# The first query weights between two blocks of x, and the last heads counted between products: one change to a gated attention kernel

## The chip, the core and the metric

The kernel runs on one core of one Trainium2 chip. The core has five engines with instruction queues of their own: TensorE (PE, with its weight loads as PEld), VectorE (DVE), ScalarE (ACT), GpSimd (POOL) and SyncE (SP, which here does nothing but issue transfers). The metric is the device time of one execution in microseconds (us), median of the runs. A profiled execution has a span, from the first to the last recorded instruction, and a little time around it that belongs to the device time too.

## What is computed

One transformer block over x of 2 x 1024 tokens and 512 features. x is normalized; 32 heads of 16 features attend causally; a base projection with a routed low-rank part (8 experts of rank 16, the best 2 of them) makes a gate; the output is x plus the product of both.

```python
xn = _layernorm(x, axis=-1)
s = _L0_attn_ref(xn, Wq, bq, Wk, bk, Wv, bv, Wo, bo)   # causal softmax attention, 32 heads of 16, then Wo
g = _silu(_L0_ffn_ref(xn, W_base, b_base, W_gate, A, B))  # base + top-2 of 8 rank-16 experts
x = x + s * g
```

## The kernel before

**Two programs in one.** `attn_gated_block` (line 79) runs `direct`, a fast path that is right as long as the softmax sums and their reciprocals stay in range. `direct` counts how many of these checks hold and leaves the count as an integer in `sound`, one number in on-chip memory. Line 93 then loads it into a register of every engine (`values_load`, one TENSOR_LOAD on each of the five queues, each waiting for `sound`), and line 94 compares it and branches: with the full count, as here, all engines jump over `general`, a slower and long program that stands between the branch and the end. The code that follows the jump is that of the end of the kernel (line 2176 in the profile): every engine drains, then they meet.

**Tiling.** Tokens are handled in chunks of C = 512 (two for each of the two sequences), each in four blocks of P = 128 tokens. Weights and heads are handled in four groups of 128 features. A unit is one sequence, one group of eight heads and one chunk of queries: 16 units, each a row of steps of scores (line 1607), exponentials (line 1618), masks on POOL (line 1635) and value products (line 1659). The steps are in `plan`, and the loop from line 1694 writes them out. `fill` puts projection work between them, from a list of tasks with costs and due times. The order on every engine is written out by this program (`manual_schedule`); each engine runs its own list strictly in order. That order is the same before and after the change, apart from what is named below.

**The start.** `x_first` holds the first four blocks of x. Lines 133 and 134 issue their loads on SP, then line 179 calls `load_qk(0)`, which loads the first group of query weights (wq) and of key weights (wk), then wv, bv and the second group follow. `first_task` (line 354) handles the four blocks: `statistics` (bn_stats, bn_aggr and a sum on DVE, a power on POOL), `normalize` on DVE, `turn` (four transposes on PE into one PSUM tile, one copy of 128 x 512 by ACT, lines 364 to 373), `project_first` (line 375, four products with wq or wk for one block). DVE's order is: statistics of blocks 0 and 1, normalize 0, statistics of 2, normalize 1, statistics of 3, normalize 2, normalize 3. PE's is: turn 0, the bias rows, queries of block 0, turn 1, keys of block 0, turn 2, queries of 1, turn 3, queries of 2 and 3, keys of 1, then the first scores. 

**The end.** The last unit ends with the last 128 queries (t = 3). `post_tile` (line 1124) transposes their heads (`pt_o`), divides by the softmax sums (`olast`) and leaves the reciprocals in `rc_last`. `turn_last` (line 1163) transposes the heads back (`pt_y`) and ACT copies them into `oT`. `whole_task` (line 1199) makes the output projection of a block, four groups k of four products with wo; `third`, the last task of this kind, does it for t = 2. `rest_task` (line 1221) does what is left for t = 3: range check into `fine`, the last group of products (line 1227), then the count: a product of `fine` with a column of ones (`pn`, line 1232), a sum and a cast to `sound` on DVE (lines 1235 and 1236). `finish_tile` (line 1192) multiplies with the gate and adds the base, both on DVE, and issues the store on SP. The end is written out in lines 1708 to 1717:

```python
    third.step()
    turn_late()
    rest.step()
    while third in tasks:
        third.step()
    active.clear()
    while late or turns or tasks:
        fill(last + 99)
```

Of the kernel before, what the change touches and what calls it, by code (L numbers as in the profile page):

```python
# [8 lines left out]
F32 = mybir.dt.float32  # L9
# [4 lines left out]
ALU = mybir.AluOpType  # L14
AX = mybir.AxisListType
# [3 lines left out]
P = 128  # L19
# [7 lines left out]
KC = D // P  # L27
# [5 lines left out]
NF = 2 + 4 * 2 * 4  # L33
# [44 lines left out]
@with_exitstack  # L78
def attn_gated_block(ctx: ExitStack, tc: tile.TileContext, *args):

    nc = tc.nc
    flag = ctx.enter_context(tc.tile_pool(name="flag", bufs=1))
    sound = flag.tile([1, 1], I32, name="sound")  # L90
    with ExitStack() as direct_ctx:
        direct(direct_ctx, tc, sound, *args)
    n = nc.values_load(sound[0:1, 0:1])
    with tc.If(n < P * NF, preferred_fallthrough_block=False):
        with ExitStack() as general_ctx:
            general(general_ctx, tc, *args)


def direct(ctx, tc, sound, x, wq, wk, wv, wo, wb, wa, wg, wB, bq, bk, bv, bo, bb, out):
# [9 lines left out]
    nc = tc.nc  # L109
    ve = Metered(nc.vector, 0.19, 966)  # L110
    act = Metered(nc.scalar, 0.22, 1274)
    sp = Queue(nc.sync)
    NB, L, _ = x.shape
    C = 512
    NC = L // C
    TT = C // P

    ctx.enter_context(tc.manual_schedule(engines=ENGINES))
    cst = ctx.enter_context(tc.tile_pool(name="cst", bufs=1))
# [5 lines left out]
    ps_av = ctx.enter_context(tc.tile_pool(name="ps_av", bufs=2, space=PSUM))  # L125
# [4 lines left out]

    x_first = chunk_tile(0, 0)
    first = [x_first[:, t] for t in range(TT)]
    for t in range(TT):
        sp.dma_start(out=first[t], in_=x[0, t * P : (t + 1) * P, :])

    def load_qk(oc):


        t = sb.tile([P, 4 * KC, P], F32, tag="wqk", bufs=2, name=f"wqk{oc}")
        for n, src in enumerate((wq, wk)):  # L140
            sp.dma_start(
                out=t[:, (2 + n) * KC : (3 + n) * KC],
                in_=src.rearrange("(kc p) o -> p kc o", p=P)[:, :, oc * P : oc * P + P],
            )
        return t

    def pair_up(t):
# [28 lines left out]
    b_rows = sb.tile([2 * KC, P], F32, tag="hl", bufs=1, name="b_rows")  # L176
    nc.scalar.dma_start(out=b_rows[0:KC], in_=bq.rearrange("(kc p) -> kc p", p=P))
    nc.scalar.dma_start(out=b_rows[KC : 2 * KC], in_=bk.rearrange("(kc p) -> kc p", p=P))
    wqks = [load_qk(0)]
    wv_sb = load_whole(wv, "wv")  # L180
    bv_sb = load_b(bv, "bv_sb")
    wqks.append(load_qk(1))
# [45 lines left out]
        rev, pattern=[[-1, E]], base=E, channel_multiplier=0,  # L228
        allow_small_or_imprecise_dtypes=True,
    )  # L230
    ones = cst.tile([P, 1], F32, name="ones")
    nc.gpsimd.memset(ones, 1.0)

    W = C // HD
# [3 lines left out]
    MM = 0.853  # L238
# [8 lines left out]
    def mm_tile(name):  # L247
        return ps_mm.tile([P, D], F32, tag="mm", name=name)
# [31 lines left out]
    def normalize(xs, mv, rstd):  # L280
        for t, xt in enumerate(xs):
            ve.tensor_scalar(
                xt, xt, mv[:, t, 0:1], rstd[:, t : t + 1], ALU.subtract, ALU.mult
            )
# [69 lines left out]
    def first_task():  # L354

        xnT = sb.tile([P, KC, C], F32, tag="xnT", bufs=3, name="xnT_0_0")
        qT = sb.tile([P, 2, C], F32, tag="qT", bufs=2, name="qT_0_0_0")
        kT = sb.tile([P, C], F32, tag="kf", bufs=2, name="kf_0_0_0")
        xnTs[0, 0], qTs[0, 0, 0] = xnT, qT
        kfs.append(kT)  # L360
        pq = ps_av.tile([P, C], F32, tag="av", name="pq_first")
        pk = ps_av.tile([P, C], F32, tag="av", name="pk_first")

        def turn(t):
            pt = mm_tile("pt_x")
            for k in range(KC):
                nc.tensor.transpose(
                    pt[:, k * P : (k + 1) * P], first[t][:, k * P : (k + 1) * P], ident
                )
            act.copy(  # L370
                xnT[:, :, t * P : (t + 1) * P], pt.rearrange("p (k t) -> p k t", k=KC)
            )
            turned_at[0, 0] = now[0] - 5

        def project_first(ps, w, t):
            cols = slice(t * P, (t + 1) * P)
            for k in range(KC):
                nc.tensor.matmul(  # L378
                    ps[:, cols], lhsT=w[:, k, :], rhs=xnT[:, k, cols], start=k == 0, stop=k == KC - 1
                )  # L380

        def queries(par):
            ve.tensor_scalar(
                qT[:, par], pq, bq_sb[:, 0:1], half[:, par : par + 1], ALU.add, ALU.mult
            )

        def keys(t0, t1):
            cols = slice(t0 * P, t1 * P)
            act.activation(kT[:, cols], pk[:, cols], AF.Identity, bias=bk_sb[:, 0:1])

        def transform(t, s):
            normalize(first[t : t + 1], *s)
            turn(t)

        s0 = yield from statistics(first[0 : 1])
        s1 = yield from statistics(first[1 : 2])
        transform(0, s0)
        b_ps = mm_tile("b_ps")[:, 0 : 2 * KC]
        nc.tensor.transpose(b_ps, b_rows, ident[0 : 2 * KC, 0 : 2 * KC])
        act.copy(b_sb, b_ps)  # L400
        s2 = yield from statistics(first[2 : 3])
        project_first(pq, wqks[0][:, 2 * KC : 3 * KC], 0)
        transform(1, s1)
        s3 = yield from statistics(first[3 : 4])
        project_first(pk, wqks[0][:, 3 * KC :], 0)
        transform(2, s2)
        project_first(pq, wqks[0][:, 2 * KC : 3 * KC], 1)
        transform(3, s3)
        room["x"] += 1
        keys(0, 1)  # L410
        project_first(pq, wqks[0][:, 2 * KC : 3 * KC], 2)
        project_first(pq, wqks[0][:, 2 * KC : 3 * KC], TT - 1)
        queries(0)
        queries(1)
        ve.stream_shuffle(b_pair, b_sb, PAIRED)
        ve.tensor_tensor(b_less, b_pair[:, 0:KC], b_pair[:, KC:], ALU.subtract)
        project_first(pk, wqks[0][:, 3 * KC :], 1)
        yield 6 * MM
        project_first(pk, wqks[0][:, 3 * KC :], 2)
        project_first(pk, wqks[0][:, 3 * KC :], 3)  # L420
        keys(1, TT)
        kTs[0, 0, 0] = sb.tile([P, 2, C], F32R, tag="kT", bufs=4, name="kT_0_0_0")
        low = sb.tile([P, C], F32, tag="rb", bufs=1, name="low_0_0_0")

        def apart():
            ve.stream_shuffle(low, kT, PAIRED)
            split_keys(kTs[0, 0, 0], low, low)
            later.append((now[0] + 1, lambda: place_keys(kTs[0, 0, 0], low)))

        later.append((0, lambda: pair_up(wqks[1])))  # L430
        paired = lambda: pair_up(wqks[0])
        costs[paired], costs[apart] = (1.1, 5), (1.1, 6)
        later.append((3, paired))
        later.append((4, apart))
        yield 2 * MM
# [49 lines left out]
    def split_keys(kT, kf, low):  # L485

        act.activation(kT, kf.unsqueeze(1).to_broadcast([P, 2, C]), AF.Copy)
        ve.tensor_tensor(low, kf, kT[:, 0].bitcast(F32), ALU.subtract)
# [663 lines left out]
    turns, turned, posts, posted, later, patient, last_out = [], [], {}, [], [], [], []  # L1152
# [16 lines left out]
    bases, whole_wo, splits, costs, urgent = {}, [], [], {}, []  # L1169
# [19 lines left out]
            ve.scalar_tensor_tensor(y, bo_sb[:, 0:BK], 0.5, g[:, BK:D], ALU.mult, ALU.mult)  # L1189
            ve.tensor_tensor(right, right, y, ALU.add)  # L1190

    def finish_tile(b, c, t, po):
        i = c * TT + t
        y = gs.pop((b, i))
        ve.scalar_tensor_tensor(y, po, 0.5, y, ALU.mult, ALU.mult)
        ve.tensor_tensor(y, y, bases[t], ALU.add)
        sp.dma_start(out=out[b, i * P : (i + 1) * P, :], in_=y)

    def whole_task(b, c, t, hold=0):

        while t not in turned or normalized(b, c) < KC - 1:
            yield WAIT
        while now[0] < hold:
            yield WAIT
        po = mm_tile("po")
        for _ in project_out(po, b, c, t, 0, KC):
            yield MM
        finish_tile(b, c, t, po)
        yield MM

    def most_task(b, c, t):
# [9 lines left out]
    def rest_task(b, c, t):  # L1221

        list(last_in_range())
        while t not in turned:
            yield WAIT
        po = mm_tile("po")
        matmul(
            po, lhsT=oTs[b, c][:, KC - 1, t * P : t * P + P], rhs=whole_wo[0][:, KC - 1],
            start=True, stop=True,
        )  # L1230
        pn = mm_tile("pn")[0:1, 0:NF]
        nc.tensor.matmul(pn, lhsT=ones, rhs=fine, start=True, stop=True)
        finish_tile(b, c, t, po)
        count = small.tile([1, 1], F32, tag="count", bufs=1, name="count")
        ve.tensor_reduce(count, pn, AX.X, ALU.add)
        ve.tensor_copy(sound, count)
        yield MM


    def in_range(ok, flat, low, high):  # L1240
# [5 lines left out]
    fine = small.tile([P, NF], F32, tag="fine", bufs=1, name="fine")  # L1246
# [123 lines left out]
    for b in range(NB):  # L1370
        for c in range(NC):
# [70 lines left out]
            else:  # L1442
                before = starts[b, KC - 1, c] + 2
                Task(len(plan) - 7, bases_task(b, c), 0.0, after=before - 12, takes={"xnT": 2})
                n = len(units) - 3
# [262 lines left out]
    third = next(x for x in tasks if x.begun)  # L1708
    rest = next(x for x in tasks if x is not third)
    third.step()  # L1710
    turn_late()
    rest.step()
    while third in tasks:
        third.step()
    active.clear()
    while late or turns or tasks:
        fill(last + 99)


def general(  # L1720
# [459 lines left out]
```

## Time and profile before

| | us |
|---|---|
| median of 3 runs | 550.99 |
| lowest, highest | 550.79, 551.87 |
| the profiled execution, device time | 551.06 |
| its span | 549.3 |
| PE, ACT, DVE, POOL busy in the span | 536.8, 351.5, 333.3, 116.6 |
| PE busy from 0 to 12 us | 9.40 |
| PE busy from 536 to 543 us | 4.83 |
| PE busy from 543 us to the end (549.3) | 0 |

The rows by stretch show where PE isn't busy: in the first 12 us it is idle for 2.6 us, in the last 13.3 us for 8.5 us, and in the 524 us between it is idle for some 1.4 us. The granted TensorE clock is 1.00 in every stretch up to 543 us. A row of the timeline gives the start (us from the span's start), the duration, engine, source line, operation and tiles; in brackets stands the idle time before it and what ended it. DVE, ACT and most POOL work shows line 56, since a helper records it; it is told apart by its tiles. The profile has 98% of the span as PE busy, where the ends of products are modelled.

### The profile page before, as it was taken

What the parts mean: (1) busy time and instruction counts of PE and PEld (TensorE: products, weight loads), DVE (VectorE), ACT (ScalarE), POOL (GpSimd) and SP (SyncE); (2) the same over time, 40 slices, a digit from 0 to 9 for tenths busy, and PEclk for the clock granted to TensorE, in tenths of its full rate; (3) what the DMA queues carried; (4) which work ended last, traced back from release to release, by engine and by line L of the source; (5) the groups of instructions that cost most, each with busy time, mean ns of one, the idle gap of its engine ahead of it and who ended that gap; (6) DMA issues with size and microseconds to landing.
All of it is one profiled execution on the core that took longest, in us unless ns stands there. A gap on an engine that the chain in (4) does not pass through costs nothing.

```text
span 549.3 us, 19455 instructions
## 1 busy us (share of the span) xinstructions
PE 536.8 (98%) x8411; PEld 278.4 (51%) x8411; DVE 333.3 (61%) x693; ACT 351.5 (64%) x389; POOL 116.6 (21%) x248
## 2 busy tenths in 40 slices
PE   8999999999999999999999999999999999999993
PEld 7435444554455544454555554454545554456651
DVE  4435586665575975566378766675086544649833
ACT  2437754776776867657666756657668776876640
POOL 2213401020134411030124321030123332020500
PEclk9999999999999999999999999999999999999998
DMA  8724357356527376713646635641133212642211
GB/s 255 187 91 158 143 161 233 98 176 196 174 98 230 126 232 217 214 42 104 210 137 195 207 111 185 186 137 45 47 111 119 82 65 54 240 157 82 97 41 47
DMA packets 66798, 78.11 MB, mean 142 GB/s; under 512 B 9880, under 2 KB 51872, under 8 KB 66064
## 3 DMA queue, kind: packets, MB, share of 16 engines
q1 hardware_dynamic: 66688, 76.78, 43.7%
q8 instruction: 68, 1.11, 0.9%
q14 instruction: 26, 0.21, 0.2%
q10 hardware_dynamic: 16, 0.00, 0.0%
HBM read 45.34 MB, written 19.37 MB: 118 GB/s over the span
## 4 chain that ended last, share of the span: by engine, by line
PE 94%; DVE 2%; ACT 1%; DMA 1%; issue 0%; SPq 0%; ACTq 0%; DVEq 0%
PE av L1659 26%; PE p L253 23%; PE s L1607 18%; PE q L253 14%; PE ph L253 3%; PE pv L253 3%; PE po L253 3%; PE pk L253 1%; PE pq L253 1%; ACT pt L56 1%; DMA wqk<-in_wq_dram 1%; PE pq_first L378 1%; PE h L253 1%; DVE g L56 1%; PE pk_first L378 1%
## 5 line engine op out<-in xcount | busy, mean ns | idle before, releaser
L56 ACT ACTIVATE pt<-s 128x1024 f32<-128x1024 f32 x288 | 290.3, 1025 | 152.0 <-PE s L1607 144.4
L1635 POOL TENSOR_SCALAR_AFFINE_SELECT pt<-pt 128x256 f32<-128x256 f32 (+1 forms) x224 | 108.6, 501 | 406.5 <-ACT pt L56 405.8
L1659 PE MATMUL av<-pt,v 128*32 128x512 f32 (+3 forms) x1680 | 155.8, 467 | 0.4 <-DVE v L56 0.2
L1607 PE MATMUL s<-qT,kT 32*128 32x512 f32 (+3 forms) x1616 | 108.3, 363 | 0.7 <-ACT pt L56 0.5
L1607 PEld LDWEIGHTS s<-qT,kT 32*128 32x128 f32 x1616 | 62.1, 183 | 59.4 <-issue 34.0
L1659 PEld LDWEIGHTS av<-pt,v 128*32 128x32 f32 x1680 | 41.1, 108 | 54.6 <-issue 38.4
L253 PE MATMUL p<-wt,asum 128*32 128x256 f32 x864 | 52.6, 379 | 0.0
L253 PE MATMUL q<-asum,wqk 128*32 128x256 f32 x832 | 51.1, 379 | 0.0
L253 PEld LDWEIGHTS p<-wt,asum 128*32 128x32 f32 x864 | 28.5, 110 | 26.4 <-issue 11.2
L253 PE MATMUL q<-xnT,wqk 128*32 128x256 f32 x624 | 39.5, 379 | 0.0
L253 PEld LDWEIGHTS q<-asum,wqk 128*32 128x32 f32 x832 | 26.8, 110 | 23.7 <-issue 7.2
L56 DVE TENSOR_TENSOR g<-p,g 128x512 f32<-128x512 f32 x20 | 13.8, 690 | 26.6 <-PE p L253 26.5
L253 PEld LDWEIGHTS q<-xnT,wqk 128*32 128x32 f32 x624 | 20.2, 110 | 18.5 <-issue 6.6
L56 DVE SCALAR_TENSOR_TENSOR kf<-q,kf 128x256 f32<-128x256 f32 x39 | 16.5, 424 | 21.3 <-PE q L253 20.6
L253 PE MATMUL p<-w,xnT 128*32 128x256 f32 x448 | 27.4, 379 | 0.0
L253 PE MATMUL p<-w,asum 128*32 128x256 f32 x320 | 20.8, 379 | 0.0
L253 PEld LDWEIGHTS p<-w,xnT 128*32 128x32 f32 x448 | 14.9, 110 | 10.6 <-issue 3.3
L253 PEld LDWEIGHTS ph<-wag_sb,xnT 128*32 128x32 f32 x512 | 15.3, 110 | 3.9 <-issue 3.0
L253 PE MATMUL po<-wo,oT 128*32 128x512 f32 x128 | 16.5, 593 | 0.4 <-ACT oT L56 0.4
L253 PE MATMUL ph<-wag_sb,xnT 128*32 128x136 f32 x512 | 16.7, 279 | 0.0
L56 DVE TENSOR_TENSOR x<-p,x 128x512 f32<-128x512 f32 x15 | 10.3, 687 | 10.3 <-PE p L253 10.2
L56 DVE TENSOR_TENSOR qT<-qf,qT 128x512 fp32r<-128x512 f32 x15 | 10.4, 697 | 9.4 <-ACT qT L56 9.4
(149 smaller groups left out, 564.8 us busy)
## 6 DMA issues: line engine op xcount, KB each, us to landing
wt<-kept SPq DMA_DIRECT2D x36, 256.0 KB
qT<-qT SPq DMA_DIRECT2D x30, 256.0 KB
x<-in_x_dram SPq DMA_DIRECT2D x16, 256.0 KB
kept<-wqk SPq DMA_DIRECT2D x16, 256.0 KB
wqk<-kept SPq DMA_DIRECT2D x4, 1024.0 KB
kT<-kf SPq DMA_DIRECT2D x30, 128.0 KB
scr<-sq SPq DMA_DIRECT2D x6, 512.0 KB
xnT<-scr SPq DMA_DIRECT2D x24, 128.0 KB
```

The costliest lines, as they stand in the source:

```text
L56: return getattr(self.engine, name)(*args, **named)
L253: nc.tensor.matmul(o[j : j + 32], lhsT=lhsT[:, j : j + 32] if len(lhsT.shape) == 2 else lhsT[:, j // 32], rhs=rhs, start=start, stop=stop,)
L378: nc.tensor.matmul(ps[:, cols], lhsT=w[:, k, :], rhs=xnT[:, k, cols], start=k == 0, stop=k == KC - 1)
L1607: nc.tensor.matmul(ss[s // 2][:, s % 2, col : col + w], lhsT=keys[rows, kt % TT * P : kt % TT * P + P], rhs=q[rows, halves * par + half_, ...
L1635: nc.gpsimd.affine_select(out=d, in_=d, compare_op=ALU.is_ge, fill=0.0, base=0, pattern=[[0, d.shape[1]], [1, P]], channel_multiplier=-1,)
L1659: nc.tensor.matmul(avs_now[par][32 * s : 32 * s + 32, q0 : q0 + w], lhsT=vs[b, kt][:, h * VS - HD * par : h * VS - HD * par + HP], rhs=pt[ ...
```

## The change

It has five edits, all in `direct` and its caller.

1. **Start, loads.** The loads of x are issued as blocks 0 and 1, then wq, then blocks 2 and 3, then wk. The rest of SP's list is as it was.
2. **Start, first turn.** For block 0 the copy by ACT is made in two halves of 128 x 256, each issued after two of the four transposes. On PE the third transpose then waits for the first half's copy, as both use one PSUM tile.
3. **End, order on PE.** After the value products, `third` makes its third group of products (k = 2), then the last heads are turned (`pt_y`), then the count is made by the new `count_fine`, then `third` makes its last group (k = 3), then the last group of t = 3. Before it was: k = 2, k = 3, turn, last group of t = 3, count. The product with ones has 32 columns of ones in place of one, and its result stands in a tile of the value products' PSUM pool; sum and cast on DVE come before the two `finish_tile`.
4. **End, loading the count.** `values_load` stands in `rest_task` ahead of its `finish_tile`, no longer behind everything. So each queue has the TENSOR_LOAD earlier: DVE between the multiplications of t = 2 and t = 3, SP between the stores of t = 2 and t = 3, PE behind its last product, ACT behind its last copy, POOL behind the sum of edit 5. The comparison and the branch stay where they were.
5. **End, one sum.** The last addition of t = 2 in `finish_tile` is made by POOL in place of DVE; the store of t = 2 waits for POOL.

```diff
-        direct(direct_ctx, tc, sound, *args)
-    n = nc.values_load(sound[0:1, 0:1])
+        n = direct(direct_ctx, tc, sound, *args)
...
-    for t in range(TT):
+
+    def load_first(t):
         sp.dma_start(out=first[t], in_=x[0, t * P : (t + 1) * P, :])
...
+            if between and not n:
+                between()
...
-    wqks = [load_qk(0)]
+    load_first(0)
+    load_first(1)
+    wqks = [load_qk(0, lambda: (load_first(2), load_first(3)))]
...
-    ones = cst.tile([P, 1], F32, name="ones")
+    ones = cst.tile([P, 32], F32, name="ones")
...
+            many = KC if t else KC // 2
             for k in range(KC):
                 nc.tensor.transpose(
                     pt[:, k * P : (k + 1) * P], first[t][:, k * P : (k + 1) * P], ident
                 )
-            act.copy(
-                xnT[:, :, t * P : (t + 1) * P], pt.rearrange("p (k t) -> p k t", k=KC)
-            )
+                if (k + 1) % many == 0:
+                    k0 = k + 1 - many
+                    act.copy(
+                        xnT[:, k0 : k + 1, t * P : (t + 1) * P],
+                        pt[:, k0 * P : (k + 1) * P].rearrange("p (k t) -> p k t", k=many),
+                    )
...
-        ve.tensor_tensor(y, y, bases[t], ALU.add)
+        (adds or ve).tensor_tensor(y, y, bases[t], ALU.add)
...
-        finish_tile(b, c, t, po)
+        finish_tile(b, c, t, po, nc.gpsimd if t == TT - 2 else None)
...
-        pn = mm_tile("pn")[0:1, 0:NF]
-        nc.tensor.matmul(pn, lhsT=ones, rhs=fine, start=True, stop=True)
+        counted.append(nc.values_load(sound[0:1, 0:1]))
         finish_tile(b, c, t, po)
+        yield MM
+
+    counted = []
+
+    def count_fine():
+        pn = ps_av.tile([P, C], F32, tag="av", name="pn")
+        nc.tensor.matmul(pn[0:32, 0:NF], lhsT=ones, rhs=fine, start=True, stop=True)
         count = small.tile([1, 1], F32, tag="count", bufs=1, name="count")
-        ve.tensor_reduce(count, pn, AX.X, ALU.add)
+        ve.tensor_reduce(count, pn[0:1, 0:NF], AX.X, ALU.add)
         ve.tensor_copy(sound, count)
-        yield MM
...
     rest.step()
+    third.step()
+    for turn in turns[:]:
+        turns.remove(turn)
+        turn[1]()
+    count_fine()
     while third in tasks:
         third.step()
     active.clear()
     while late or turns or tasks:
         fill(last + 99)
+    return counted[0]
```

More of the change, by code (lines that the diff above doesn't have):

```diff
@@ L132, in direct, with load_qk @@
     first = [x_first[:, t] for t in range(TT)]
-    for t in range(TT):
+    def load_first(t):
         sp.dma_start(out=first[t], in_=x[0, t * P : (t + 1) * P, :])
-    def load_qk(oc):
+    def load_qk(oc, between=None):
         t = sb.tile([P, 4 * KC, P], F32, tag="wqk", bufs=2, name=f"wqk{oc}")
@@ L1190, in bases_task, with finish_tile @@
             ve.tensor_tensor(right, right, y, ALU.add)
-    def finish_tile(b, c, t, po):
+    def finish_tile(b, c, t, po, adds=None):
         i = c * TT + t
```

## The prediction

> **What bounds the kernel now.** I read the page first: busy times and the chain of waits.
>
> ```profile
> PE 536.8 (98%) x8411; PEld 278.4 (51%) x8411; DVE 333.3 (61%) x693; ACT 351.5 (64%) x389; POOL 116.6 (21%) x248
> ...
> PE 94%; DVE 2%; ACT 1%; DMA 1%; issue 0%; SPq 0%; ACTq 0%; DVEq 0%
> ```
>
> PE carries the chain, and the windows by stretch have it busy all but some 1.4 us between 12 and 536 us. The lists of all engines are unchanged there, so a shift of the start reaches the end nearly whole, and nothing else in the middle can pay. What can change is the first 12 us and the last 13. The timeline of the start (start us, duration us, engine, operation):
>
> ```profile
> 6.06 0.69 DVE L56 BATCH_NORM_STATS2 st<-x 128x6 f32<-128x512 f32 x1
> ...
> 7.07 0.54 DVE L56 TENSOR_SCALAR x<-x,mv,rstd 128x512 f32<-128x512 f32 x1
> 7.52 0.68 DVE L56 BATCH_NORM_STATS2 st<-x 128x6 f32<-128x512 f32 x1
> 8.13 1.13 PE L378 MATMUL pq_first<-xnT,wqk 128*128 128x128 f32 x8 [1.12 <-DMA wqk<-in_wq_dram]
> ...
> 9.10 0.60 PE L367 MATMUL pt_x<-ident,x 128*128 128x128 f32 x4
> ...
> 10.43 0.60 PE L367 MATMUL pt_x<-ident,x 128*128 128x128 f32 x4
> ```
>
> PE stands 1.12 us for wq, the fifth 256 KB in SP's queue. At 6.06 DVE takes the statistics of block 2, and only behind them, at 7.07, normalizes block 1, which PE turns at 9.10. The timeline of the end:
>
> ```profile
> 537.61 1.90 PE L253 MATMUL po<-wo,oT 128*32 128x512 f32 x16
> ...
> 539.32 0.40 PE L253 MATMUL pt_y<-ident,olast 128*32 128x128 f32 x8
> ...
> 539.57 0.69 DVE L56 SCALAR_TENSOR_TENSOR g<-po,g 128x512 f32<-128x512 f32 x1 [0.96 <-PE po L253]
> 539.79 0.27 ACT L56 COPY oT<-pt_y 128x128 f32<-128x128 f32 x1 [4.43 <-PE pt_y L253]
> ...
> 540.11 1.06 PE L253 MATMUL po<-wo,oT 128*32 128x512 f32 x8 [0.39 <-ACT oT L56]
> 540.30 0.69 DVE L56 TENSOR_TENSOR g<-g,x_last 128x512 f32<-128x512 f32 x1
> ...
> 541.97 0.69 DVE L56 TENSOR_TENSOR g<-g,x_last 128x512 f32<-128x512 f32 x1
> 542.58 0.17 DVE L56 TENSOR_REDUCE count<-pn 1x1 f32<-1x34 f32 x1
> 542.79 0.14 DVE L56 CAST sound<-count 1x1 int32<-1x1 f32 x1
> ```
>
> The count is ready at 542.93, and still the span runs to 549.3. The rows of the branch line and of the closing line say why (count, duration ns min/median/max, first and last start):
>
> ```profile
> L94 DVEq COMPARE_BRANCH  x2: 51/53/55, 543.6 to 543.8; - x2
> L94 ACTq COMPARE_BRANCH  x2: 38/44/49, 543.8 to 543.9; - x2
> ```
>
> ```profile
> L2176 DVEq DRAIN  x2: 10/26/41, 548.0 to 548.8; - x2
> L2176 ACTq DRAIN  x2: 8/44/81, 548.4 to 548.8; - x2
> ```
>
> All engines load the count at 543.0 (0.46 to 0.55 us) and take the jump at 543.7 (POOL), 543.8 (DVE), 543.9 (PE and ACT). The first instruction behind it starts at 547.7, 548.0, 547.4 and 548.4: 4.0, 4.25, 3.5 and 4.5 us of nothing but instruction packets. SP's jump, at 544.8, takes 0.2. So the end is: each engine's jump, plus about 4 us, plus 0.85 us from the last drain (548.43) to the span's end.
>
> **The change, part by part.**
>
> Loads. By the trace's completions (sixteen a transfer) the third transfer in the queue lands by 5.83, the fourth by 7.25 (all but one of its sixteen by 6.82), the fifth by 8.00, the sixth by 8.74. All are 256 KB; a 2 KB packet takes 104 ns, a 512 B packet of wq 27, so places keep their times. wq moves to the third place, 2.2 us earlier. But block 2 moves to the fourth, L = 7.25 in place of 5.83, and it is the next in DVE's list: its statistics start at L + 0.02 = 7.27 and not at 6.06. From there the rows give the spacing: normalize 1 is 1.01 later (8.28 to 8.82; PE waits for it from 8.6 on), statistics of 3 are 1.46 after the first (8.73; block 3 landed by 8.00), normalize 2 another 1.01 on (9.74 to 10.28), and turn 2 starts at 10.33 where it started at 10.43. wk (sixth, 8.74, unmoved) is needed at 9.3. So of the 1.12 us only **0.10** arrive; the wait moves from PE to DVE. Ends: with L = 6.82, 0.5 (PE's own order then binds: see the next part); with L = 7.6, a loss of 0.25.
>
> First turn. Copies of 128 x 512 (0.59) and 128 x 128 (0.37) put 128 x 256 at 0.44. Two transposes, first copy 6.67 to 7.12, third and fourth transposes, second copy 7.62 to 8.06, products of block 0 done near 8.58: later than an unsplit copy would give with wq there, yet ahead of 8.82. Cost **0** while block 1 is late; if L falls under about 7.0, this is what holds turn 1 at 8.6.
>
> Order at the end. The third group ends at 538.47; olast was ready at 538.31, so the turn runs there (PE 0.22 in this place: 539.32 to the next product would have been so much), then the count's product (0.23; `fine` is ready at 538.61), then the last group: 538.93 to 539.79 instead of 538.47 to 539.32. ACT's copy comes 0.47 after the turn's start, 538.94 to 539.21, so PE no longer waits 0.39 for it: the last products start at 539.79 for 540.11. DVE multiplies t = 2 at 540.04 for 539.57, and t = 3 1.13 after the last products' start, at 540.92 for 541.24. Sum and cast are done near 539.45, in DVE's idle time (0.96 before 539.57). Wider ones: the weight load stays below the 0.11 us rows; nothing.
>
> Loading the count. On DVE 0.54 us of load stand between the two multiplications; the first runs 540.04 to 540.73. If the queue loads while the engine works it costs nothing, if not t = 3 starts at 541.28. No row shows which; loads sit in the queue, like waits, so I take 0 (ends 0 and 0.36). [...]
>
> The sum on POOL. It starts at 540.73 + 0.1 (handoffs before POOL's powers are 0.09 to 0.16) = 540.83. No sum of 128 x 512 on POOL is in the trace. The nearest row, a mask of 128 x 512 with one input, takes 0.69 on average; then POOL is done at 541.52, before DVE's last sum (0.73 after 540.92, at 541.65) begins. [...]
>
> ```profile
> 514.55 0.97 POOL L1635 TENSOR_SCALAR_AFFINE_SELECT pt<-pt 128x512 f32<-128x512 f32 x1 [0.40 <-ACT pt L56]
> ...
> 515.06 1.00 DVE L56 TENSOR_TENSOR x<-x,xr 128x512 f32<-128x512 f32 x1
> ```
>
> The same sum takes 0.69 where POOL is idle. [...]
>
> Jumps. ACT's and PE's come near 540.5 and 541.3, POOL's at 542.1, DVE's 0.15 behind its last sum, at 542.82 instead of 543.78: sum, cast and load no longer stand behind it. DVE is last. Its gap: 4.25 in its own row, 3.5 in PE's (shortest), 4.5 in ACT's, where four engines fetch together; spread out I take 4.0. Drain 546.82, end 547.67 against 549.3: **1.65** (2.15 to 1.15 by the gap's ends; 0.35 more if POOL is quick, 0.36 less if DVE's load isn't hidden).
>
> Sum: 551.06 - 0.10 - 1.65 = **549.3**. The profiled execution lies 0.07 above the median, which changes nothing.
>
> **Rivals.** (a) More arrives: L = 6.82 (0.5) and a gap of 3.5 (2.15): 548.4. For it: one straggler of sixteen makes 7.25. (b) The gap isn't counted from each jump but from the last store: the instruction packets start at 544.4, just as its data stop, and the jumps are too close together to tell. [...] Against it: SP's fetch needs nothing of the kind. (c) The start loses: a straggler holds block 2 until 8.0, where the fifth transfer's is; 0.65 lost, 550.1. [...]
>
> **How the numbers follow.** Forecast 0.58 (own range 548.7 to 549.9), (a) 0.16, (b) 0.11, (c) 0.08, (d) 0.07. A measurement tells some 0.2%, 1.1 us, from no change: forecast and (a) are faster, (b) and (c) the same, (d) slower. The range goes from (a)'s 548.3 to past (c), 550.3.
>
> **What would show it.** Start: no wait of PE for wq, statistics of block 2 at about 7.3 with DVE idle for the DMA, turn 2 within 0.3 us of 10.4. End: last products at 539.8; the POOL sum at 1.1 to 1.2 us and DVE's last sum held to about 542.0; jumps spread from 540.5 to 542.8; last drain that of DVE near 546.8. I am wrong if ACT and PE, jumping 2 us before DVE, still drain after 547, or if the POOL sum takes over 2 us.

## The result, and the profile after

| | before | after |
|---|---|---|
| median of 6 runs, us | 551.05 | 549.18 |
| lowest, highest | 550.79, 551.87 | 548.74, 549.29 |
| the profiled execution, span | 551.06, 549.3 | 548.74, 547.0 |

The medians differ by 1.87 us (0.34%); the ratio of the runs is 0.9962, with a 95% interval from 0.9952 to 0.9973. The forecast was 549.3.

The page of the changed kernel, its busy times and its chain:

```profile
PE 537.0 (98%) x8411; PEld 278.5 (51%) x8411; DVE 332.8 (61%) x692; ACT 351.6 (64%) x390; POOL 117.4 (21%) x249
...
PE 96%; DVE 2%; ACT 1%; issue 0%; POOL 0%; ACTq 0%; POOLq 0%; DVEq 0%
```

PE does the same work in a shorter span. The timeline of the start, as shown of before:

```profile
6.67 0.69 DVE L56 BATCH_NORM_STATS2 st<-x 128x6 f32<-128x512 f32 x1 [0.63 <-DMA x<-in_x_dram]
...
7.31 0.44 PE L372 MATMUL pt_x<-ident,x 128*128 128x128 f32 x2 [0.46 <-ACT xnT L56]
7.69 0.54 DVE L56 TENSOR_SCALAR x<-x,mv,rstd 128x512 f32<-128x512 f32 x1
...
7.83 1.16 PE L386 MATMUL pq_first<-xnT,wqk 128*128 128x128 f32 x8
...
10.16 0.60 PE L372 MATMUL pt_x<-ident,x 128*128 128x128 f32 x4
```

PE no longer waits for wq, and DVE waits for block 2 instead. A new wait of PE stands in the second row: the third transpose of block 0 waits 0.46 us for ACT to copy the first half. Turn 2 starts at 10.16 (10.43 before). The timeline of the end:

```profile
538.13 0.41 PE L257 MATMUL pt_y<-ident,olast 128*32 128x128 f32 x8
...
538.34 0.21 PE L1247 MATMUL pn<-fine,ones 128*32 128x34 f32 x1
...
538.36 0.62 PE L257 MATMUL po<-wo,oT 128*32 128x512 f32 x3
...
538.64 0.18 DVE L56 TENSOR_REDUCE count<-pn 1x1 f32<-1x34 f32 x1 [0.36 <-PE pn L1247]
...
539.53 0.69 DVE L56 SCALAR_TENSOR_TENSOR g<-po,g 128x512 f32<-128x512 f32 x1 [0.54 <-PE po L257]
540.31 1.26 POOL L1204 TENSOR_TENSOR g<-g,x_last 128x512 f32<-128x512 f32 x1 [11.15 <-DVE g L56]
540.39 0.69 DVE L56 SCALAR_TENSOR_TENSOR g<-po,g 128x512 f32<-128x512 f32 x1 [0.17 <-PE po L257]
541.12 1.00 DVE L56 TENSOR_TENSOR g<-g,x_last 128x512 f32<-128x512 f32 x1
```

The products run on without a wait. In what follows a transfer has *landed* with the last of the sixteen completions that it reports, a *jump* runs from an engine's second branch to its first instruction behind it, and an *instruction packet* is a DMA packet that the trace lists under the kind *instruction* (94 in the changed kernel, 1.32 MB). The rows by line of the branch and of the program's last line, where the closing code stands (count, duration ns min/median/max, first and last start):

```profile
L93 SPq EVENT_SEMAPHORE  x8: 17/17/17, 543.3 to 545.4; - x8
L93 ACTq COMPARE_BRANCH  x2: 38/44/49, 539.6 to 539.7; - x2
...
L93 DVEq COMPARE_BRANCH  x2: 51/53/55, 541.1 to 542.3; - x2
L93 SPq COMPARE_BRANCH  x2: 38/46/53, 543.2 to 545.5; - x2
```

```profile
L2195 SPq EVENT_SEMAPHORE  x10: 17/28/28, 545.7 to 546.9; - x10
...
L2195 SPq DRAIN  x3: 7/7/7, 546.2 to 546.5; - x3
L2195 ACTq DRAIN  x2: 8/44/81, 542.2 to 546.5; - x2
...
L2195 DVEq DRAIN  x2: 10/26/41, 545.4 to 546.5; - x2
```

On each engine but SP the first drain is the first instruction behind the jump. ACT is there at 542.2, 2.5 us after its second branch, DVE at 545.4, 3.2 after. The last is **SP, at 546.2**: it stands until the last store has landed (545.40), takes its second branch at 545.5, is through its jump at 545.7, and makes eight checks of semaphores before it drains. In before, SP drained at 545.5, some 3 us ahead of ACT.

The span is 2.26 us shorter; this execution is the fastest of its six, and the second profile of the changed kernel, below, has 1.95. From the rows: turn 2 is 0.27 earlier, which is 0.34 at the last exponentials; from the start of the last `pt_o` row to that of the last single product 2.66 us pass, where it was 3.19 (0.53); and from the start of that product to the end of the span 7.30, where it was 8.69 (1.39). This last stretch is called **the tail** below.

### The profile page after: what moved, and what is told of

Read it like the earlier page. It is cut to its first block, busy times and chain, and to the rows that moved or that the text cites. A ratio compares the mean times of both kernels' runs of the same rounds, so it can differ in the third digit from the quotient of the medians.

```text
span 547.0 us, 19459 instructions
## 1 busy us (share of the span) xinstructions
PE 537.0 (98%) x8411; PEld 278.5 (51%) x8411; DVE 332.8 (61%) x692; ACT 351.6 (64%) x390; POOL 117.4 (21%) x249
## 4 chain that ended last, share of the span: by engine, by line
PE 96%; DVE 2%; ACT 1%; issue 0%; POOL 0%; ACTq 0%; POOLq 0%; DVEq 0%
PE av L1672 26%; PE p L257 23%; PE s L1620 18%; PE q L257 14%; PE ph L257 3%; PE pv L257 3%; PE po L257 2%; PE pk L257 1%; PE pq L257 1%; ACT pt L56 1%; PE warm L212 1%; PE pq_first L386 1%; PE h L257 1%; DVE g L56 1%; PE pk_first L386 1%
```

## The experiments

Twelve runs, each beside the kernel before on the same chip (its medians there: 550.86 to 550.97). A single run has no interval. Edits 3 and 4 were not run apart; what each is worth is read from the rows. "Statistics" is the start of those of block 2, "scores" that of the first scores, both in the profiled execution.

| run | median us (runs) | ratio to before, 95% interval | statistics | scores | span | tail |
|---|---|---|---|---|---|---|
| before | 551.05 (6) | | 6.06 | 15.18 | 549.3 | 8.69 |
| before again | 551.12 (1) | | 6.13 | 15.22 | 549.3 | 8.59 |
| start alone | 550.26 (20) | 0.9990 (0.9983 to 0.9997) | 7.30 | 15.24 | 548.7 | 8.09 |
| loads alone | 550.95 (13) | 0.9997 (0.9989 to 1.0005) | 7.41 | 15.34 | 549.3 | 8.48 |
| halves alone | 550.39 (14) | 0.9992 (0.9983 to 1.0001) | 6.56 | 15.18 | 548.6 | 8.00 |
| end alone | 549.54 (9) | 0.9975 (0.9965 to 0.9985) | 6.65 | 15.37 | 547.8 | 7.35 |
| after | 549.18 (6) | 0.9962 (0.9952 to 0.9973) | 6.67 | 14.90 | 547.0 | 7.30 |
| after again | 549.12 (6) | 0.9966 (0.9955 to 0.9978) | 7.21 | 15.15 | 547.3 | 7.34 |
| one copy | 548.78 (1) | | 6.68 | 14.75 | 547.0 | 7.46 |
| two banks | 548.82 (7) | 0.9965 (0.9952 to 0.9978) | 6.58 | 14.51 | 546.8 | 7.30 |
| load behind | 549.06 (5) | 0.9961 (0.9947 to 0.9975) | 6.59 | 15.18 | 547.1 | 7.11 |
| sum on DVE | 549.01 (7) | 0.9969 (0.9957 to 0.9980) | 6.56 | 14.75 | 546.9 | 7.39 |
| banks, behind | 548.90 (6) | 0.9967 (0.9955 to 0.9979) | 7.18 | 15.11 | 547.0 | 7.14 |
| no jump | 547.38 (4) | 0.9934 (0.9917 to 0.9950) | 7.29 | 15.23 | 545.6 | 5.46 |

### Each end of the change alone

The first run has edits 1 and 2 (the order of the loads, the two half copies), the second edits 3 to 5.

> The start's two edits alone (order of loads, first copy in halves) on the kernel before. Theory, from the changed kernel's trace: turn 2 starts some 0.27 us earlier (10.16 for 10.43) and this reaches the end whole: device time 0.2 to 0.4 us below before, no measurable difference, the end unchanged (last drain 0.85 us ahead of the span's end, ACT's). The prediction's sum: 0.10 us. Rival: the start gives more than the trace of one execution shows, over 1 us, and the end less.

> The end's three edits alone (order on PE, load of the count, sum on POOL), the start as before. Theory: 1.8 to 2.1 us below before, span near 547.3. The prediction's sum: 1.65 us. Rival (the start carries the gain): under 1 us.

The end alone is worth most of it: 549.54, 1.3 below before, less than the 1.8 to 2.1 expected, with a tail of 7.35, and SP drains last there too. The start alone gave 0.6, more than expected and not where it was expected: in its profile the scores start no earlier than before. Its tail is 0.6 shorter, and there nothing was edited.

### Which of the two start edits shortens the tail

Each start edit was run alone, and before a second time, to see whether 8.7 is an accident of one execution.

```diff
# loads alone, against before
-    for t in range(TT):
+    def load_first(t):
...
-    wqks = [load_qk(0)]
+    load_first(0)
+    load_first(1)
+    wqks = [load_qk(0, lambda: (load_first(2), load_first(3)))]
# halves alone, against before
+            many = KC if t else KC // 2
...
-            act.copy(
+                if (k + 1) % many == 0:
...
```

> The kernel before once more, for a second profile. Theory (the wait behind the jump differs between executions, 8.69 us from the last product's start to the end in the first profile and 8.09 in the start-alone kernel, whose end is the same code): between 8.0 and 8.7, with block 2 landed at 5.8 and the fourth transfer between 6.6 and 7.3. Rival (the gap belongs to how the code lies): 8.7 again within 0.1.

> The kernel before with block 0's normalized half copied in two halves, nothing else; the transfers stay in their old order. Theory (the stretch after the last product depends on how the code lies before the jumps, and one ACT instruction more with one PE wait fewer is enough to shift it): nothing at the start, span end about 8.1 after the start of the last product, as in the run with the two start edits alone, and a time 0.4 to 0.6 below the kernel before. Rival (the 0.6 of that run came from the order of the transfers, or from chance): 8.6 to 8.7 after the last product, and the same time as before within 0.15.

> The kernel before with wq fetched between blocks 1 and 2, the copy whole; the instructions of ACT and PE are as before. Theory (code position decides the tail): 8.6 to 8.7 from the last product to the end of the span, a gain at the start alone, 0 to 0.5 by the landing of the fourth transfer (6.6 or 7.3), so a time 0.1 to 0.4 below before. Rival (the order of the transfers is what e1 gained by): the whole 0.6, with the scores 0.5 earlier in most executions.

The halves shorten the tail as expected, the loads don't (nor do they give the 0.1 to 0.4 us expected of them), and before repeats its long one (8.59), as the rival had it. The rows by line, the branch and the last line, with the loads alone:

```profile
L94 ACTq COMPARE_BRANCH  x2: 38/44/49, 544.0 to 544.2; - x2
```

```profile
L2181 ACTq DRAIN  x2: 8/44/80, 548.5 to 548.8; - x2
...
L2181 DVEq DRAIN  x2: 10/25/40, 548.2 to 548.9; - x2
```

and with the halves alone:

```profile
L94 ACTq COMPARE_BRANCH  x2: 38/44/49, 543.5 to 543.6; - x2
```

```profile
L2180 ACTq DRAIN  x2: 8/44/81, 546.7 to 548.1; - x2
...
L2180 DVEq DRAIN  x2: 10/25/40, 547.8 to 548.1; - x2
```

ACT loads the count at 543.21 in the first run and at 542.94 in the second, for 0.47 us each. With the whole copy its first branch starts 0.35 after that load, with the halves 0.06; then it takes 4.3 us from its second branch to its drain, against 3.1 (4.0 in the run of both start edits). With the whole copy ACT is the last to drain, with the halves DVE is, and DVE too comes a little sooner. In the first us after the last store's data six instruction packets start with the whole copy (one of 8 KB took 1.60 us; 2.06 and 1.75 in the two profiles of before), five with the halves. The pause goes with the halves in all thirteen traces with a jump: it is 0.35 in the five with one copy (before twice, loads alone, end alone, one copy), and 0.06 in the eight with halves. The halves add one ACT instruction 530 us earlier: 703 of ACT's are recorded ahead of its first branch in the five, 704 in the eight. The traces show the pause and the packets, not what ties them to the copy, and no run adds an instruction that does nothing else, so the cause stays open. The jump takes 2.4 to 4.5 us on ACT, DVE, POOL and PE, with packets in flight, and 0.2 on SP.

By time alone the halves' 0.58 us is just not certain (the interval ends at 1.0001); the run of both start edits (0.9990, up to 0.9997) and the tails of the profiles (8.00 and 8.09 against 8.48 to 8.69) support it. In the changed kernel it pays nothing, as ACT jumps 2.5 us before DVE: with one copy there ACT drains at 543.0 and not at 542.2, and SP still ends the span.

### What holds the start

```diff
# one copy: the changed kernel with a copy of 128x512 for block 0
# two banks: the changed kernel with the halves in two tiles
-            pt = mm_tile("pt_x")
+            pt = mm_tile("pt_x") if t else None
...
+                if not t and k % many == 0:
+                    pt = ps_s.tile([P, 2, C], F32, tag="s", name="pt_x")[:, 0]
```

> The changed kernel with one copy of 128 x 512 for block 0 in place of two halves that wait for each other on one PSUM tile. Theory (the halves stand in line: PE waits 0.46 us between second and third transpose): the products of block 0 start no later than with halves (7.83), turn 1 between 8.5 and 8.8 (8.83 with halves), so the halves gain nothing. Rival: the products of block 0 start 0.3 us later, and turn 1 with them, near 9.1.

> The changed kernel with the two halves of block 0 in two PSUM tiles, so that the third transpose doesn't wait for the first copy. Theory: four transposes in a row, second copy done near 7.7, products of block 0 done near 8.2; turn 1 then waits for normalize 1 alone (8.23 in the changed kernel's trace, with block 2 landed at 6.65), turn 2 follows normalize 2 (9.70): 0.4 us earlier than the changed kernel where block 2 lands by 6.7, nothing where it lands at 7.3. Time 0 to 0.4 us below the changed kernel. Rival (block 2's landing binds always): 0.0.

The timeline of the start with two banks:

```profile
6.25 0.66 PE L374 MATMUL pt_x<-ident,x 128*128 128x128 f32 x4 [0.30 <-DVE x L56]
...
6.73 0.65 ACT L56 COPY xnT<-pt_x 128x256 f32<-128x256 f32 x2 [3.77 <-PE pt_x L374]
7.15 0.97 PEld L388 LDWEIGHTS pq_first<-xnT,wqk 128*128 128x128 f32 x8 [0.18 <-ACT xnT L56]
```

Four transposes run through, the copies overlap them, and the first products start 0.90 after the first transpose. With the halves in one tile that takes 1.37 (6.46 to 7.83), since the third transpose writes into the tile that ACT reads; with one copy 1.33 (6.35 to 7.68). So edit 2 gains nothing at the start as written, and in two tiles the first products come 0.4 us sooner. In time two banks lie 0.3 below the changed kernel, which these intervals don't separate.

### The jumps and the stores

This run leaves out the fallback: no load of the count, no branch, no general program.

```diff
-        n = direct(direct_ctx, tc, sound, *args)
-    with tc.If(n < P * NF, preferred_fallthrough_block=False):
-        with ExitStack() as general_ctx:
-            general(general_ctx, tc, *args)
+        direct(direct_ctx, tc, sound, *args)
...
-        counted.append(nc.values_load(sound[0:1, 0:1]))
+        counted.append(None)
```

> The changed kernel without the load, the jump and the general program (it leaves out the fallback for sums out of range; the count is still made). No instruction fetch by a jump is left. Theory (fetch packets of the early jumps hold DMA engines while the last two stores move: 2.85 and 2.75 us from issue to landing, 2.0 before): both stores land 2.0 us after issue again, the last is issued near 542.2 and lands near 544.2, the span is 1.0 to 1.4 us shorter than the changed kernel's. Rival (the two stores slow each other): landings stay at 2.7 to 2.9 us and the span is 0.4 us shorter.

The tail is 1.84 shorter than in the changed kernel, the span 1.45 (block 2 landed late, at 7.27); 1.0 to 1.4 was expected. Along SP: the last store is issued 2.44 after the last product and not 2.95 (its load of the count is gone, 0.51), it lands 2.14 after its issue and not 2.74 (0.60), and the drain follows 0.11 after the landing and not 0.80 (0.69: there is no jump, and SP has made all but the last of its closing checks by then). The windows of one us show the stores; a row has the stretch, its length, the busy time (and number) of PE, PEld, DVE, ACT and POOL, PE's clock, and last the share of the DMA engines' time and GB/s. First the changed kernel, then the one without jumps:

```profile
542.00:543.00 1.00, 0.00 (x0) 0.00 (x0) 0.12 (x1) 0.00 (x0) 0.00 (x0) 1.00 0.57 199
543.00:544.00 1.00, 0.00 (x0) 0.00 (x0) 0.00 (x0) 0.00 (x0) 0.00 (x0) 1.00 0.57 203
544.00:545.00 1.00, 0.00 (x0) 0.00 (x0) 0.00 (x0) 0.00 (x0) 0.00 (x0) 1.00 0.55 180
```

```profile
542.00:543.00 1.00, 0.00 (x0) 0.00 (x0) 0.51 (x1) 0.00 (x0) 0.00 (x0) 1.00 0.18 68
543.00:544.00 1.00, 0.00 (x0) 0.00 (x0) 0.00 (x0) 0.00 (x0) 0.00 (x0) 1.00 1.01 379
544.00:545.00 1.00, 0.00 (x0) 0.00 (x0) 0.00 (x0) 0.00 (x0) 0.00 (x0) 1.00 0.21 78
```

Without jumps two stores, issued 0.55 apart, move at 379 GB/s and land 2.06 and 2.14 after their issue, against 2.0 in before; so the rival, that they slow one another, falls. In the changed kernel, issued 1.06 apart, they land after 2.85 and 2.74. Of the sixteen parts of a store the first comes 1.87 after the issue of the first store, as before (1.84), the last 0.98 behind it, where it was 0.17. So some of the sixteen are late: the last three come 0.31 to 0.84 behind the other thirteen. Five instruction packets (four of 8 KB at 0.31 to 0.64 us, one of 16 KB at 1.19) fly from 540.6 to 543.9, and more from 544.6; before, they began at 544.45, when the stores' data were through. The delay goes when load and jump go. It is not SP's load of the count, since the store is as late when that load stands behind it (3.07, next run). So it comes with the jumps; what makes the last parts late no trace shows.

### The last store earlier, two ways

The first run moves the load of the count behind the last store in SP's queue (and behind the last sum in DVE's), the second puts the sum of t = 2 back on DVE.

```diff
# load behind, against the changed kernel
-        counted.append(nc.values_load(sound[0:1, 0:1]))
         finish_tile(b, c, t, po)
+        counted.append(nc.values_load(sound[0:1, 0:1]))
# sum on DVE, against the changed kernel
-        finish_tile(b, c, t, po, nc.gpsimd if t == TT - 2 else None)
+        finish_tile(b, c, t, po)
```

> The changed kernel with the load of the count behind the last finish_tile, so that SP issues the last store before its TENSOR_LOAD. Theory (SP's last store sets the end: issued at 542.65 behind the load, landed at 545.40): the store is issued near 542.2, lands 0.45 us earlier, the span is 0.3 to 0.5 us shorter than the changed kernel's 547.0 relative to the last products on PE. Rival, the prediction's (DVE's jump sets the end): the last drain is DVE's and the end doesn't move, 0.0 to 0.1 us.

> The changed kernel with the last sum of t = 2 back on DVE. Theory (POOL's sum keeps the two last stores late and POOL's own jump among them, so it earns nothing): store of t = 2 issued near 541.0, POOL jumps near 540, DVE's last sum takes 0.69 and ends 0.3 later than with POOL (1.00, 542.12), the last store is issued within 0.2 of 542.65 but lands up to 0.7 earlier; span 0.0 to 0.7 us shorter. Rival, the reason for the edit (DVE's row is what the last store waits for): last store and span 0.3 us later.

Behind the last sum the load lets the store go 2.43 after the last product, 0.51 earlier; it lands 3.07 after its issue, and 0.19 of the half microsecond is left in the tail, under the 0.3 to 0.5 expected. With the sum on DVE the rows of the timeline are

```profile
540.74 0.69 DVE L56 SCALAR_TENSOR_TENSOR g<-po,g 128x512 f32<-128x512 f32 x1
541.46 0.69 DVE L56 TENSOR_TENSOR g<-g,x_last 128x512 f32<-128x512 f32 x1
```

The last sum takes 0.69 and not 1.00 but starts behind one more sum; it ends 2.61 after the last product, 2.41 with POOL. The store of t = 2 is issued 1.27 after the last product and not 1.89, and takes 3.66 us; that of t = 3, at 2.64, takes 3.14. Both kernels end alike, with neither the gain expected nor the rival's loss of 0.3: edit 5 earns nothing that can be seen. In the eight traces with jumps and the new end, the last store lands 5.50 to 5.85 after the last product, whether issued at 2.43 or at 2.95; without jumps at 4.58.

### Both improvements, and the changed kernel again

> The changed kernel with block 0's halves in two PSUM tiles and the sound flag loaded behind the last store. Theory: the halves no longer wait for one another, the scores start near 14.5 (14.9 in the changed kernel), the tail stays at 7.1 to 7.3: 0.2 to 0.4 below the changed kernel run again beside it, about 548.8. Rival: the landing of block 2 and the length of the warm-up products differ by more than that from one execution to the next, and the two are the same within 0.15.

> The changed kernel once more, as measure for the run beside it. Theory: 549.2 within 0.2, about 1.9 below before; the last store lands 2.7 to 2.9 after its issue and SP drains last, 7.3 after the start of the last product. Rival (the longer landing was an accident of one execution): landing near 2.0 and an end with DVE, near 6.5 to 7.0.

The changed kernel again gives 549.12. The kernel with both lies 0.22 below, with nearly the same interval: the two can't be told apart, and the 0.2 to 0.4 expected is not shown. In these two profiles block 2 landed at 7.1 to 7.2, and then the banks don't matter. The timeline of the changed kernel's second profile:

```profile
7.21 0.69 DVE L56 BATCH_NORM_STATS2 st<-x 128x6 f32<-128x512 f32 x1 [1.22 <-DMA x<-in_x_dram]
...
8.91 0.63 PE L372 MATMUL pt_x<-ident,x 128*128 128x128 f32 x4 [0.23 <-DVE x L56]
...
10.37 0.63 PE L372 MATMUL pt_x<-ident,x 128*128 128x128 f32 x4
```

This is the forecast's start: 7.27, then turn 2 at 10.33. The span is 547.3, 0.3 more than in the first profile, and the store again lands 2.78 after its issue. No version is shown to beat the changed kernel, save the one without fallback, which is another program.

## Why the prediction was right

**Start.** The wait that takes over was right; what it pays was not. L is the landing of block 2. In the ten profiles with the new order of loads, L falls in two groups. At 7.15 to 7.38, the forecast's case, turn 2 starts at 10.34 to 10.57 in five profiles: no gain on the 10.43 and 10.47 of before, where 0.10 was forecast. At 6.54 to 6.66 it starts at 9.74 to 10.44 in the other five, two of which have another first turn. The first profile is one of these, with L = 6.65, below the lower end of 6.82 that the forecast gave 0.5: its scores are 0.28 earlier, those of the second (L = 7.18) 0.03. As foreseen for an early L, the first turn then holds turn 1. The wait between the halves was in the working, and its length is right: turn 1 starts 2.36 after turn 0 (forecast 8.6, less the 6.20 of before). But turn 0 starts at 6.46, behind products on the identity (line 208 before, 212 after) that stand ahead of it on PE. First before, then after:

```profile
3.72 2.42 PE L208 MATMUL warm<-ident 128*128 128x128 f32 x14
```

```profile
3.72 2.91 PE L212 MATMUL warm<-ident 128*128 128x128 f32 x14
```

The same fourteen take 0.49 longer, at a granted clock of 1.00 in both. With the load behind the last store they end later still: turn 0 starts at 6.70, and turn 2 at 10.44 in spite of L = 6.57. The working has no term for this, and its cause stays open. What the start is worth on average stays open as well: the loads alone gain nothing (550.95 against 550.97), while the end without the start edits is 0.4 behind the changed kernel, with intervals that overlap; in its one profile the third transfer, block 2, landed at 6.63 and not at 5.83, so that its scores come late.

**Order at the end.** Right in direction, mis-sized: 0.53 for 0.32. The term was the count's product, put at 0.23 from the row of before, where no product follows it. In the changed kernel the next products start 0.02 behind it (538.34 and 538.36). Whether the 32 columns, costed at "nothing", or the place of the product brings this is open, since no run has one column there.

**Loads of the count.** Right: DVE's load runs from 539.54 to 540.09, inside the multiplication of 539.53 to 540.22. SP's load, in front of the last store, delays its issue by 0.51 us (2.95 after the last product, 2.43 with the load behind the store); 0.19 of that came back at the end.

**The sum on POOL.** DVE's jump at 542.82 is added up from two terms that no run shows: 1.1 to 1.2 us for this sum, and a last sum on DVE held until POOL's has ended. The runs show 1.26 (1.27 without jumps) on POOL, and DVE's last sum, started 0.45 before POOL's ended, took 1.00, where it takes 0.69 with the other sum on DVE, and ended 0.55 behind POOL's. The prediction's own rows had this: the mask ends at 515.52, the sum at 516.06, 0.54 later. The two misses cancel: from the last product's start DVE's sum ends at 2.41, as forecast.

**Jumps and end: the step that failed.** The forecast had "DVE is last", a gap of 4.0 and a drain at 546.82; SP, with its store and its drain, has no term in that sum. The gap was mis-sized: DVE 3.2, POOL 2.7, ACT 2.5, PE 3.7 (before 4.25, 4.0, 4.5, 3.5). In the eight profiles of the new end, where the jumps are spread out, DVE, POOL and ACT take 2.4 to 3.5, and 3.1 to 4.5 in the five of the old end; PE takes 3.4 to 3.9 and 3.4 to 3.7, with a packet of 16 KB some 1 us after its second branch. The last store took 2.74 us from issue to landing, where it took 2.0 in before. So the two engines changed places. From the last product's start DVE's drain comes after 5.72 (forecast 6.56) and SP's after 6.49 (4.91 in before). That the later of the two is within 0.1 of the forecast's 6.56 is luck: the tail's number was right with the wrong engine at its end, and the total is better than its parts.

**Rivals.** (b), the gap counted from the last store, falls: ACT drains at 542.2, before that store is issued. Yet it had hold of something real, for the store and SP's jump and checks behind it now set the end. Of the two signs of being wrong that were named neither came: ACT and PE drained at 542.2 and 544.2, not after 547, and POOL's sum took 1.26, not over 2 us. (d), a slower kernel, did not occur. (c) did not occur; block 2 landed at 7.4 at the latest. (a) is half of the first profile: the early landing came, DVE's quick gap came too, but SP hid it.

## What to carry to other kernels

When several waits end within a microsecond, removing the last one shows the next: follow each queue to its own end, SP's with issue, landing and jump, before naming the engine that ends the span. Here jumps that were spread out were quicker, save PE's (2.4 to 3.5 us on DVE, POOL and ACT, 3.1 to 4.5 where they came together), and the stores beneath them slower; a store's time from a quiet stretch of the trace (2.0) did not hold there (2.74 and 2.85). When an edit gains time far from its own place, as here 0.6 us at the branch from a copy at the start, run each half of the edit alone, and look at the pauses around the branch.

## What was not expected of the hardware

- The fourth transfer of 256 KB lands early (6.54 to 6.66 in six traces) or late (7.15 to 7.38 in eight), whichever tensor it carries. A start edit worth 0.3 us is of the size of this spread.
- One ACT copy split in two at the start of the kernel went with 0.6 us less at its end (a tail of 8.00, against 8.59 and 8.69 in before).
- A store of 256 KB took 2.0 us on its own and 2.74 to 3.66 while instruction packets of 8 and 16 KB were in flight.
- The same fourteen products on the identity took 2.42 us in one execution and 2.91 in another, at the same granted clock.
- DVE took the load of a register (0.55 us) while its previous instruction was at work.
